# A four-layer graph network on one core: own rows gathered inside layer 2's tile loop, and the check of the softmax's bound moved ahead of the last tile's closing

## The chip, the core and the metric

The kernel runs on 1 core of one Trainium2 chip. A core has four engines that compute, TensorE (PE in the profile, with PEld for its weight loads), VectorE (DVE), ScalarE (ACT) and GpSimd (POOL), and SyncE (SP), which here only starts transfers. Each engine works through its own list of instructions in order; semaphores hold an instruction until what it needs is there. The metric is the device time of one execution in microseconds (us), and a kernel's time is the median over its runs. Beside the timed runs there is one execution under the profiler; all durations and starts below come from that one, and starts count from the beginning of its span.

## The reference

3125 nodes with 128 features, 100000 edges sorted by their destination. Four layers, each `x = layernorm(x + layer(x))`. The change lies in the third of them, which the kernel calls layer 2, an attention over each node's incoming edges with 4 heads of 32 features:

```python
Q = (x @ Wq).reshape(n, H, HD); K = (x @ Wk).reshape(n, H, HD); V = (x @ Wv).reshape(n, H, HD)
attn = jnp.sum(Q[dst] * K[src], axis=-1) * SCALE + edge_attr @ We
attn = jnp.where(attn >= 0, attn, 0.2 * attn)
attn_exp = jnp.exp(attn - jnp.max(attn))
attn_sum = jax.ops.segment_sum(attn_exp, dst, num_segments=n)
attn_norm = attn_exp / jnp.maximum(attn_sum[dst], 1e-12)
agg = jax.ops.segment_sum(V[src] * attn_norm[:, :, None], dst, num_segments=n)
agg = agg.reshape(n, H * HD) @ Wo + bo
return relu(jnp.concatenate([x, agg], axis=1) @ Wm + bm)
```

Two things in it matter here. The exponential is taken against one maximum over all edges and heads, and the sum has a floor of 1e-12. The layer behind it, layer 3, is again an attention over the edges, in which each edge uses a key that depends on its type (8 types) and on its source node.

## The kernel before

**Tiles.** The nodes are ordered by their number of incoming edges and cut into 25 tiles (`NT`) of 128, one node per partition. Tile t holds `CAP[t]` edge slots per node, from 57 for tile 0, then 42, 40, 39 down to 21 for the last: 821 slots in all (`NS`). The slots are worked on in chunks of 8 (`W`), and several chunks make a segment with one softmax update (`segments`); tile 0 has two segments. Edges beyond a node's slots would be handled by an overflow loop (`behind`, L641 to L667), a loop with a trip count that is read at run time (L647). With this data it makes no trip. Its head (L648) is a barrier of all engines, at which outstanding transfers are waited for as well.

**Tables.** The layer before leaves two tables in DRAM: `xq_tab`, for each node its own features and its query (256 floats), and `kv_tab`, key and value (256 floats). `pay_sb` holds for every slot the source node, the edge's type and its three attributes; it is loaded at L1124 in one transfer of 2463 KB on SP's queue. `xqb` keeps own features (`xb`) and queries (`qb`) of all 25 tiles in SBUF; layer 3 uses both halves as layer 2 has rewritten them.

**Gathers.** Every gather is an indirect DMA issued by POOL (helper `gather`, L90): one instruction fetches 128 rows, one per partition, from a table by a column of indices. Scatters (`scatter`, L93, through `put`, L736) go the same way.

**Layer 2, in the order of the source** (L1118 to L1277):

- `accb`, the accumulator of all tiles, is cleared (L1134), and the 25 gathers of own rows into `xqb` follow (L1135 to L1136).
- The overflow loop (`behind(wp, behind2)`), and behind it the loads of the weights.
- For each tile: `query` (L706) copies the tile's queries into PSUM. For each chunk `rows2` issues 8 gathers into `kv`, which has 8 buffers, multiplies keys by queries on DVE (`qk`, L1143) and sums over the features (L1144). `biased` (L1147 to L1155) adds the edges' bias, `softmax` (L670 to L687) updates a running maximum `m` and sum `l` of each node and head, `faded` (L691) rescales the accumulator, and `weigh` (L693 to L701) multiplies the values by the weights (`msg`, L696), sums over the slots (`u`, L700) and adds to the accumulator (L701).
- `closing(t, rl)` (L1186 to L1204): accumulator over sum (`an`), transposed on PE (L711), times `wo` (`o_ps`, L1194), own features transposed (L711), both times `wm` (`h_ps`, L1199 and L1200), `y` (L1202, L1203) and the layernorm (L717 to L729), which writes the new features into `xb`.
- `table3(t)` (L1206 to L1224): queries, keys and values of layer 3, and for each of the 8 edge types the transformed key (`e_ps`, L1221; `rows`, L1222); one scatter of 128 rows of 8 KB into `ktv_tab` ends it (L1224, by L93).
- After all tiles the check. The kernel normalizes by a maximum per node and head instead of the one over everything, so the floor of 1e-12 might apply in the reference where it doesn't here. The check takes the maximum of `m` over everything (`mx_all`, transposed on PE at L1252, `top`, L1254), scales the sums to it (`f`, L1256 and L1257; L1260), counts the sums that lie under the floor (`few`, L1262 to L1266, by a matmul over the partitions) and reads the count into a register of every engine (L1268, L1269). If it is above 0 (L1270), all tiles are closed again. With this data it is 0.

Layer 3 (from L1279) has the same shape: memsets, an overflow loop with its barrier, then gathers from `ktv_tab` and a loop over the tiles.

**What sets the order.** The source gives the data flow, and tile pools give the buffers (two of each name unless `bufs` says otherwise; in PSUM one). A scheduler places each engine's instructions; their order on an engine is then fixed and need not be that of the source.

Of the kernel before, what the change touches and what calls it, by code (L numbers as in the profile page):

```python
# [18 lines left out]
P = 128  # L19
N = 3125  # L20
NT = 25
# [38 lines left out]
def segments(t):  # L60

    cs = chunks(t)
    n = -(-len(cs) // 5)
    runs = [cs[i * len(cs) // n:(i + 1) * len(cs) // n] for i in range(n)]
    return [(run[0][0], sum(run[-1]), run) for run in runs]
# [10 lines left out]
def tile_gnn(ctx, tc, a, out):  # L76
    nc = tc.nc
    V, A, G, T = nc.vector, nc.scalar, nc.gpsimd, nc.tensor
# [10 lines left out]
    def gather(dst, table, idx, **kw):  # L89
        return G.indirect_dma_start(out=dst, out_offset=None, in_=table, in_offset=indirect(idx), **kw)  # L90
# [10 lines left out]
    ident = const.tile([P, P], F32, name="ident")  # L101
# [5 lines left out]
    ones = const.tile([P, P], F32, name="ones")  # L107
# [355 lines left out]
    od = Order("d", order_d)  # L463
# [21 lines left out]
    with tc.tile_pool(name="srcp", bufs=1) as sp, tc.tile_pool(name="srcq", bufs=2, space=PSUM) as ps:  # L485
# [8 lines left out]
        for t in range(NT):  # L494
# [245 lines left out]
    xq_tab = dram.tile([NP, 2 * D], F32, name="xq_tab")  # L740
# [7 lines left out]
    with tc.tile_pool(name="l0", bufs=2) as wp, tc.tile_pool(name="l0s", bufs=1) as sp, \  # L748
# [243 lines left out]
    with ExitStack() as ctx1, tc.tile_pool(name="l1", bufs=2) as wp, tc.tile_pool(name="l1s", bufs=1) as sp:  # L992
# [71 lines left out]
        ps1 = ctx1.enter_context(tc.tile_pool(name="l1p", bufs=1, space=PSUM))  # L1064
# [53 lines left out]
    H2 = 4  # L1118
    big = ctx.enter_context(tc.tile_pool(name="big", bufs=1))
    xqb = big.tile([P, NT, 2 * D], F32, name="xqb")  # L1120
# [4 lines left out]
    with tc.tile_pool(name="l2", bufs=2) as wp, tc.tile_pool(name="l2s", bufs=1) as sp, \  # L1125
# [6 lines left out]
        l = sp.tile([P, NT, H2], F32, name="l")  # L1132
        V.memset(l, 0.0)
        V.memset(accb, 0.0)  # L1134
        for t in range(NT):  # L1135
            gather(xqb[:, t, :], xq_tab, od.ids(t))  # L1136

        def rows2(qp, pl, n, lg):
            kv = wp.tile([P, W, 2 * D], F32, name="kv", bufs=8)
            for s in range(n):  # L1140
                gather(kv[:, s, :], kv_tab, pl[:, s, 0:1])
            qk = wp.tile([P, W, D], F32, name="qk")
            V.tensor_mul(qk[:, :n], kv[:, :n, :D], qp.unsqueeze(1).to_broadcast([P, n, D]))  # L1143
            V.tensor_reduce(lg, qk[:, :n].rearrange("p s (h d) -> p s h d", h=H2), AX.X, OP.add)  # L1144
            return kv
# [10 lines left out]

        def behind2(t, pl, mk, rl):
            lg = wp.tile([P, max(CAP), H2], F32, name="lg")
            kv = rows2(query(ps1, qb[:, t, :]), pl, W, lg[:, :W])
            biased(pl, W, lg[:, :W], mk)  # L1160
            ex = ps1.tile([P, max(CAP), H2], F32, name="ex")
            corr = softmax(wp, lg[:, :W], W, H2, m[:, t, :], l[:, t, :], ex[:, :W])
            faded(accb[:, t, :], corr, H2)
            weigh(wp, accb[:, t, :], kv[:, :, D:], ex[:, :W], W, H2)
# [21 lines left out]
        def closing(t, scale):  # L1186

            an = wp.tile([P, D], F32, name="an")
            V.tensor_tensor(an.rearrange("p (h d) -> p h d", h=H2),
                            accb[:, t, :].rearrange("p (h d) -> p h d", h=H2),  # L1190
                            scale.unsqueeze(2).to_broadcast([P, H2, D // H2]), op=OP.mult)
            aT = transposed(wp, ps1, an, "aT")
            o_ps = ps1.tile([P, P], F32, name="o_ps", tag="dense")
            T.matmul(o_ps, wo, aT, start=True, stop=True)  # L1194
            oT = wp.tile([P, P], F32, name="oT")
            A.activation(oT, o_ps, AF.Identity, bias=bo)
            xT = transposed(wp, ps1, xb[:, t, :], "xT")
            h_ps = ps1.tile([P, D], F32, name="h_ps", tag="dense")
            T.matmul(h_ps, xT, wm[:, 0, :], start=True, stop=False)  # L1199
            T.matmul(h_ps, oT, wm[:, 1, :], start=False, stop=True)  # L1200
            y = wp.tile([P, D], F32, name="y")
            V.tensor_add(y, h_ps, bm)  # L1202
            V.scalar_tensor_tensor(y, y, 0.0, xb[:, t, :], op0=OP.max, op1=OP.add)  # L1203
            layernorm(wp, xb[:, t, :], y, t)  # L1204

        def table3(t):  # L1206
# [16 lines left out]
            A.activation(rows[:, :, D:], qkv[:, 2 * D:].unsqueeze(1).to_broadcast([P, NET, D]), AF.Copy)  # L1223
            put(ktv_tab, od, t, rows.rearrange("p e f -> p (e f)"))  # L1224

        for t in range(NT):
            qp = query(ps1, qb[:, t, :])
            for s0, s1, run in segments(t):
                lg = wp.tile([P, max(CAP), H2], F32, name="lg")
                parts = []  # L1230
                for c0, w in run:
                    o = OFF[t] + c0
                    parts.append(rows2(qp, pay_sb[:, o:o + w], w, lg[:, c0 - s0:c0 - s0 + w]))
                n, o = s1 - s0, OFF[t] + s0
                biased(pay_sb[:, o:o + n], n, lg[:, :n], mask[:, o:o + n])
                ex = ps1.tile([P, max(CAP), H2], F32, name="ex")
                corr = softmax(wp, lg[:, :n], n, H2, m[:, t, :], l[:, t, :], ex[:, :n])
                faded(accb[:, t, :], corr, H2)
                for (c0, w), kv in zip(run, parts):
                    weigh(wp, accb[:, t, :], kv[:, :w, D:], ex[:, c0 - s0:c0 - s0 + w], w, H2)  # L1240

            rl = wp.tile([P, H2], F32, name="rl")
            V.tensor_scalar(rl, l[:, t, :], 1e-12, None, op0=OP.max)
            V.reciprocal(rl, rl)
            closing(t, rl)
            table3(t)


        mx = sp.tile([P, 1], F32, name="mx_all")
        V.tensor_reduce(mx, m, AX.XY, OP.max)  # L1250
        mt = ps1.tile([P, P], F32, name="tp")
        T.transpose(mt, mx.to_broadcast([P, P]), ident)  # L1252
        top = sp.tile([P, 1], F32, name="top")
        V.tensor_reduce(top, mt, AX.X, OP.max)  # L1254
        f = sp.tile([P, NT, H2], F32, name="f")
        V.tensor_scalar(f, m, top, None, op0=OP.subtract)  # L1256
        A.activation(f, f, AF.Exp)  # L1257
        has2 = sp.tile([P, NT, H2], F32, name="has2")
        V.tensor_scalar(has2, l, 0.0, None, op0=OP.is_gt)
        V.tensor_mul(l, l, f)  # L1260
        few = sp.tile([P, NT, H2], F32, name="few")
        V.scalar_tensor_tensor(few, l, 1e-12, has2, op0=OP.is_lt, op1=OP.mult)  # L1262
        few1 = sp.tile([P, 1], F32, name="few1")
        V.tensor_reduce(few1, few, AX.XY, OP.add)
        few_ps = ps1.tile([1, 1], F32, name="few_ps", tag="tp")
        T.matmul(few_ps, few1, ones[:, :1], start=True, stop=True)  # L1266
        fewi = sp.tile([1, 1], I32, name="fewi")
        V.tensor_copy(fewi, few_ps)  # L1268
        again = nc.values_load(fewi, min_val=0, max_val=NP * H2)  # L1269
        with tc.If(again > 0):  # L1270
            V.tensor_scalar(l, l, 1e-12, None, op0=OP.max)
# [78 lines left out]
```

## Time and profile before

| | |
|---|---|
| time, median of 3 runs | 5862.23 us |
| the runs | 5864.28, 5854.55, 5862.23 us |
| the profiled execution | 5814.11 us |
| its span | 5812.4 us |
| mean clock granted to TensorE | 0.588 of full speed |
| PE / PEld busy | 2236.2 us (38%) / 1363.8 us (23%) |
| ACT busy | 934.1 us (16%) |
| gathers of own rows in layer 2 | 25, from 3223.3 to 3253.4 us, 943 to 989 ns each |
| edge gathers of layer 2 | 821, from 3262.7 to 4503.6 us, median 947 ns |
| layer 3's edge gathers begin | 4592.45 us |

The page of a profile begins with the busy time of each engine. A chain of waits follows back from the last instruction: at each step to what released it, or to the instruction before it on its engine; "issue" in it is time in which an engine waited for nothing that the profile shows. Groups of instructions are given by line, engine, operation and tile, as `out<-in`; behind the bar stands the time that the engine was idle before them and what ended most of it. In a timeline each instruction has its start, its duration, engine, line and operation; the brackets hold the idle time of its engine just before and the releaser. The duration of an indirect DMA on POOL is that of making its descriptors; the data land later. The profiled execution is 48 us shorter than the median of the timed runs, so a difference of a few microseconds is read within one trace, not between a trace and a time.

### The profile page before, as it was taken

To read this page: it belongs to the slowest core of one execution; us is meant where nothing else is said; L and a number is where in the kernel's file an instruction comes from. 1 tells how busy PE (TensorE), PEld (TensorE's weight loads), DVE (VectorE), ACT (ScalarE), POOL (GpSimd) and SP (SyncE) were. 2 spreads that over 40 slices of the span, in tenths; PEclk is the share of its full clock that TensorE was granted. 3 is DMA by queue.
4 is the path that set the end of the run, shared out by engine and by line. 5 is a ranking of instruction groups with operands and counts; after the bars stand their busy time and mean duration, and the time that the engine had idled before them with its cause. 6 is when DMAs were issued, how large, how long until landed. Compare 5 with 4: busy or idle time off the path is not lost. (4 is left out here: it accounts for less than half of the span.)

```text
span 5812.4 us, 36204 instructions
## 1 busy us (share of the span) xinstructions
PE 2236.2 (38%) x10027; PEld 1363.8 (23%) x10027; DVE 3104.1 (53%) x6976; ACT 934.1 (16%) x2437; POOL 3074.3 (53%) x3136
## 2 busy tenths in 40 slices
PE   7165545555556556576658112222233200000000
PEld 5143333333334334344433001111111100000000
DVE  8354555554455446565652346565656455545555
ACT  1031222221222222222211001111111100000000
POOL 0555545545453544444640566566656366666664
PEclk9565556555665666566569555555555555555555
DMA  2423322322222222222335333333333233333332
GB/s 80 120 75 85 88 75 76 86 74 80 74 81 70 80 76 79 82 76 79 102 92 196 106 95 107 99 110 114 104 100 107 72 96 92 90 93 93 94 89 66
DMA packets 220239, 530.60 MB, mean 91 GB/s; under 512 B 65690, under 2 KB 112461, under 8 KB 215386
## 3 DMA queue, kind: packets, MB, share of 16 engines
q0 software_dynamic: 147968, 437.97, 26.6%
q1 hardware_dynamic: 72024, 89.90, 4.7%
q8 instruction: 87, 1.43, 0.1%
q14 instruction: 160, 1.30, 0.1%
HBM read 457.09 MB, written 70.63 MB: 91 GB/s over the span
## 5 line engine op out<-in xcount | busy, mean ns | idle before, releaser
L90 POOL DMA_INDIRECT hs<-h_tab,srcx x821 | 880.0, 1072 | 602.1 <-issue 448.7
L90 POOL DMA_INDIRECT kv<-kv_tab,pay_sb x821 | 782.1, 953 | 421.7 <-issue 239.5
L90 POOL DMA_INDIRECT kv<-ktv_tab,pay_sb x821 | 778.8, 949 | 332.3 <-issue 258.1
L90 POOL DMA_INDIRECT zs<-z_tab,rel x445 | 466.8, 1049 | 695.4 <-DVE az L810 303.3
L628 PE MATMUL c_ps<-c_ohs,c_ohd 128*128 128x128 bf16 x1300 | 334.3, 410 | 299.1 <-issue 110.3
L700 DVE TENSOR_REDUCE u<-msg 128x128 f32<-128x1024 f32 (+4 forms) x228 | 384.2, 1685 | 114.3 <-remote 69.6
L838 PE MATMUL zps<-oh,zq 128*128 128x512 bf16 x752 | 339.7, 516 | 88.3 <-DVE oh L834 80.1
L790 PE MATMUL lg<-yw,low 128*128 128x8 f32 x1642 | 306.4, 316 | 125.8 <-ACT low L788 81.6
L790 PEld LDWEIGHTS lg<-yw,low 128*128 128x128 f32 x1642 | 305.2, 276 | 162.8 <-ACT low L788 104.0
L628 PEld LDWEIGHTS <-c_ohd 128*128 128x128 bf16 x1300 | 187.2, 147 | 431.7 <-issue 256.2
L1295 DVE TENSOR_TENSOR qk<-kv,qp 128x1024 f32<-128x1024 f32 (+4 forms) x114 | 126.4, 1109 | 289.1 <-DMA kv<-ktv_tab,pay_sb 242.8
L623 DVE TENSOR_TENSOR c_ohs<-c_ends,c_up 128x1024 bf16<-128x1024 bf16 (+4 forms) x193 | 118.9, 616 | 248.0 <-remote 111.8
L696 DVE TENSOR_TENSOR msg<-kv,ex 128x1024 f32<-128x1024 f32 (+4 forms) x228 | 249.1, 1104 | 0.0
L604 ACT ACTIVATE c_oha<-c_oha,srclo 128x50 bf16<-128x50 bf16 (+2 forms) x821 | 201.5, 327 | 258.8 <-DVE c_oha L600 189.5
L850 DVE TENSOR_TENSOR hs<-hs,t_ps 128x408 f32<-128x408 f32 x141 | 74.5, 528 | 300.2 <-remote 193.0
L787 DVE TENSOR_TENSOR low<-pre,h1T 128x512 f32<-128x512 f32 (+1 forms) x215 | 141.3, 660 | 166.9 <-PE pre L843 76.1
L630 ACT ACTIVATE c_sb<-c_ps 128x512 bf16<-128x512 f32 (+1 forms) x175 | 96.5, 552 | 802.2 <-remote 363.0
L1143 DVE TENSOR_TENSOR qk<-kv,qp 128x1024 f32<-128x1024 f32 (+4 forms) x114 | 126.1, 1107 | 181.6 <-DMA kv<-kv_tab,pay_sb 173.1
L849 PE MATMUL t_ps<-zw,zT 128*128 128x136 f32 x752 | 153.7, 338 | 151.1 <-issue 105.1
L711 PE MATMUL tp<-ident,xk 128*128 128x128 f32 x100 | 42.3, 423 | 426.7 <-DVE xk L1211 88.6
L711 PE MATMUL tp<-ident,an 128*128 128x128 f32 x25 | 11.5, 461 | 434.5 <-DVE msg L696 174.3
L788 ACT ACTIVATE low<-low 128x512 f32<-128x512 f32 (+1 forms) x215 | 128.9, 606 | 274.7 <-DVE low L787 246.1
(394 smaller groups left out, 5252.7 us busy)
## 6 DMA issues: line engine op xcount, KB each, us to landing
c_tab<-c_sb SPq DMA_DIRECT2D x25, 768.0 KB
cs<-c_tab SPq DMA_DIRECT2D x6, 3200.0 KB
hs<-h_tab,srcx POOLq DMA_INDIRECT x821
kv<-kv_tab,pay_sb POOLq DMA_INDIRECT x821
kv<-ktv_tab,pay_sb POOLq DMA_INDIRECT x821
rb<-rel_tab SPq DMA_DIRECT2D x47, 256.0 KB
zs<-z_tab,rel POOLq DMA_INDIRECT x445
h_tab<-h SPq DMA_DIRECT2D x25, 132.0 KB
```

The lines of the kernel that those rows point to most:

```text
L90: return G.indirect_dma_start(out=dst, out_offset=None, in_=table, in_offset=indirect(idx), **kw)
L604: A.activation(oha[:, s, 0, :], oha[:, s, 1, :], AF.Copy, scale=srclo[:, o:o + 1])
L628: T.matmul(cps[:, j * P:(j + 1) * P], ohd[:, :, nb * j + i], ohs[:, :, nb * j + i], start=(i == 0), stop=(i == nb - 1))
L696: V.tensor_tensor(msg[:, :n, :].rearrange("p s (h d) -> p s h d", h=heads), val.rearrange("p s (h d) -> p s h d", h=heads), ex.unsqueeze(3 ...
L700: V.tensor_reduce(u, msg[:, :n, :].rearrange("p s d -> p d s"), AX.X, OP.add)
L787: V.tensor_add(low[:, :k], pre[:, :k], h1T.unsqueeze(1).to_broadcast([P, k, P]))
L788: A.activation(low[:, :k], low[:, :k], AF.Relu)
L790: T.matmul(lg_ps[:, s, :], low[:, s, :], yw8, start=True, stop=True)
L838: T.matmul(z, w, oh[:, i], start=(whole and i == 0), stop=(whole and i == NK - 1))
L849: T.matmul(t_ps[:, s, :], zT[:, (s0 + s) * P:(s0 + s + 1) * P], zw[:, D:], start=True, stop=True)
L1143: V.tensor_mul(qk[:, :n], kv[:, :n, :D], qp.unsqueeze(1).to_broadcast([P, n, D]))
L1295: V.tensor_mul(qk[:, :n], kv[:, :n, :D], qp.unsqueeze(1).to_broadcast([P, n, D]))
```

## The change

The 25 gathers of own rows leave the place in front of the overflow loop. In the tile loop the rows of tile 0 are gathered ahead of the loop, and those of tile t + 1 behind the query of tile t; the body of the overflow loop, which makes no trip here, gets its own gather. The check becomes a function and is called in the last tile's turn, behind its sums and in front of its `closing`; its operations are the same.

```diff
         V.memset(accb, 0.0)
-        for t in range(NT):
-            gather(xqb[:, t, :], xq_tab, od.ids(t))
-
...
         def behind2(t, pl, mk, rl):
             lg = wp.tile([P, max(CAP), H2], F32, name="lg")
+            gather(xqb[:, t, :], xq_tab, od.ids(t))
             kv = rows2(query(ps1, qb[:, t, :]), pl, W, lg[:, :W])
...
+        def check():
+
+            mx = sp.tile([P, 1], F32, name="mx_all")
+            V.tensor_reduce(mx, m, AX.XY, OP.max)
+            mt = ps1.tile([P, P], F32, name="tp")
+            T.transpose(mt, mx.to_broadcast([P, P]), ident)
...
+            T.matmul(few_ps, few1, ones[:, :1], start=True, stop=True)
+            fewi = sp.tile([1, 1], I32, name="fewi")
+            V.tensor_copy(fewi, few_ps)
+            return f, fewi
+
+        gather(xqb[:, 0, :], xq_tab, od.ids(0))
         for t in range(NT):
             qp = query(ps1, qb[:, t, :])
+            if t + 1 < NT:
+                gather(xqb[:, t + 1, :], xq_tab, od.ids(t + 1))
             for s0, s1, run in segments(t):
...
             V.reciprocal(rl, rl)
+            if t == NT - 1:
+                f, fewi = check()
             closing(t, rl)
             table3(t)
 
-
-        mx = sp.tile([P, 1], F32, name="mx_all")
-        V.tensor_reduce(mx, m, AX.XY, OP.max)
...
-        fewi = sp.tile([1, 1], I32, name="fewi")
-        V.tensor_copy(fewi, few_ps)
         again = nc.values_load(fewi, min_val=0, max_val=NP * H2)
```

More of the change, by code (lines that the diff above doesn't have):

```diff
@@ L1224, in table3 @@
             put(ktv_tab, od, t, rows.rearrange("p e f -> p (e f)"))
+        def check():
[3 more added lines that the diff above has]
+            T.transpose(mt, mx.to_broadcast([P, P]), ident)
+            top = sp.tile([P, 1], F32, name="top")
+            V.tensor_reduce(top, mt, AX.X, OP.max)
+            f = sp.tile([P, NT, H2], F32, name="f")
+            V.tensor_scalar(f, m, top, None, op0=OP.subtract)
+            A.activation(f, f, AF.Exp)
+            has2 = sp.tile([P, NT, H2], F32, name="has2")
+            V.tensor_scalar(has2, l, 0.0, None, op0=OP.is_gt)
+            V.tensor_mul(l, l, f)
+            few = sp.tile([P, NT, H2], F32, name="few")
+            V.scalar_tensor_tensor(few, l, 1e-12, has2, op0=OP.is_lt, op1=OP.mult)
+            few1 = sp.tile([P, 1], F32, name="few1")
+            V.tensor_reduce(few1, few, AX.XY, OP.add)
+            few_ps = ps1.tile([1, 1], F32, name="few_ps", tag="tp")
+            T.matmul(few_ps, few1, ones[:, :1], start=True, stop=True)
[3 more added lines that the diff above has]
+        gather(xqb[:, 0, :], xq_tab, od.ids(0))
         for t in range(NT):
             qp = query(ps1, qb[:, t, :])
+            if t + 1 < NT:
+                gather(xqb[:, t + 1, :], xq_tab, od.ids(t + 1))
             for s0, s1, run in segments(t):
@@ L1244, in tile_gnn @@
             V.reciprocal(rl, rl)
+            if t == NT - 1:
+                f, fewi = check()
             closing(t, rl)
             table3(t)
-        mx = sp.tile([P, 1], F32, name="mx_all")
-        V.tensor_reduce(mx, m, AX.XY, OP.max)
[L1251 to L1266, printed above, removed]
-        fewi = sp.tile([1, 1], I32, name="fewi")
-        V.tensor_copy(fewi, few_ps)
         again = nc.values_load(fewi, min_val=0, max_val=NP * H2)
```

## The prediction

> **What bounds the kernel now.** I read the page's head first, then the timeline of the start of layer 2, the wait of its barrier, and the timelines of the places that the diff touches. All times are us from the start of the span.
>
> ```profile
> span 5812.4 us, 36204 instructions
> ...
> PE 2236.2 (38%) x10027; PEld 1363.8 (23%) x10027; DVE 3104.1 (53%) x6976; ACT 934.1 (16%) x2437; POOL 3074.3 (53%) x3136
> ...
> POOL 12%; DVE 12%; issue 12%; another core or an unknown queue 5%; PE 2%; DMA 1%; ACT 1%; DVEq 0%; POOLq 0%; ACTq 0%
> ...
> L90 POOL DMA_INDIRECT kv<-kv_tab,pay_sb x821 | 782.1, 953 | 421.7 <-issue 239.5
> ```
>
> No engine is full: POOL, which issues every gather, and DVE have 53% each, and the chain that ended last goes back and forth between them. A layer-2 gather costs POOL 0.953 us and 0.3 us up to the next one (239.5 us over 786), 1.25 us in all. The change touches the start of layer 2 and its last tile, so I look there.
>
> The timeline of layer 2's start (start, duration, engine, line, what; in brackets the idle time before it and its releaser):
>
> ```profile
> 3222.52 0.32 SPq L1124 DMA_DIRECT2D pay_sb<-pay_tab  x1
> 3223.15 2.73 DVE L1134 MEMSET accb<- 128x3200 f32 x1 [3.16 <-DMA kv_tab<-kv]
> 3223.33 0.99 POOL L90 DMA_INDIRECT xqb<-xq_tab,node_d  x1 [174.73 <-issue]
> 3224.63 0.97 POOL L90 DMA_INDIRECT xqb<-xq_tab,node_d  x1 [0.30 <-issue]
> ...
> 3253.44 0.96 POOL L90 DMA_INDIRECT xqb<-xq_tab,node_d  x1 [0.30 <-issue]
> ...
> 3259.56 0.94 DVE L1149 TENSOR_TENSOR eb<-pay_sb,we 128x384 f32<-128x384 f32 x2 [33.56 <-issue]
> ...
> 3262.68 0.94 POOL L90 DMA_INDIRECT kv<-kv_tab,pay_sb  x1 [8.28 <-DVE eb L1149]
> ```
>
> The 25 gathers of own rows run from 3223.33, one per 1.25 us, to 3254.4. DVE has been idle for 33.6 us when it goes on at 3259.56, and the first edge gather starts at 3262.68. What held them is the barrier at the head of the overflow loop (L648), in the view of waits; and the stretches beside it show when the big load of `pay_sb` has drained (length, then busy us and counts of PE, PEld, DVE, ACT and POOL, PE's clock, the DMA share, GB/s):
>
> ```profile
> SPq L648 <- DMA xqb<-xq_tab,node_d: 35.1, 1, 35.1
> ```
> ```profile
> 3230.00:3232.00 2.00, 0.00 (x0) 0.00 (x0) 0.00 (x0) 0.00 (x0) 1.55 (x2) 0.50 0.87 328
> ...
> 3240.00:3256.00 16.00, 0.00 (x0) 0.00 (x0) 0.00 (x0) 0.00 (x0) 11.04 (x12) 0.50 0.36 107
> ```
>
> SP's queue waits 35.1 us for the landing of own rows. `pay_sb` (2463 KB, issued at 3222.52) holds the DMA engines at 0.87 until about 3232, after which they fall to the 0.36 that own rows alone make: it has landed by about 3232.
>
> **Part 1, own rows.** The order of instructions says more than the source. The scheduler does not place one gather per tile: behind the barrier POOL now issues 12 gathers of own rows, 57 edge gathers, 1 of own rows, 32 edge gathers, 12 of own rows, 50 edge gathers, then tile 0's scatter (L93). Before, the scatter followed 139 edge gathers. Everything behind that scatter keeps its order on POOL, and DVE, ACT, PE and SP keep theirs in the whole loop but for the last tile. The number of gathers that run is the same.
>
> Removed: the barrier's wait for own rows. What is late next is `pay_sb`, which POOL needs for its indices: 3232, plus what POOL takes to its first DMA. The bounds are 0.3 us, its usual step, and the 3.1 us by which it left the barrier later than DVE (3262.68 − 3259.56); I take 0.9, nearer the first, because the exit can be done while the load still runs. First own-row gather at 3232.9 (3232.3 to 3235.1). Twelve at 1.25 make 15.0: the first edge gather starts at 3247.9 instead of 3262.68, **14.8 us earlier** (12.6 to 15.4). If the barrier holds for `pay_sb` as well, add the 6.5 us that lie between about 3256.2 (own rows landed: 3253.44 plus some 2.7) and 3262.68: 3238.5, so 9.2 earlier; that is the lower bound.
>
> Added in the stream: one gather behind the 57th, 1.25 us, on the path, since tile 0's products wait for data (see the line at 3365.78 below, 7.39 us of waiting): left **13.5 us**. Twelve more behind the 89th, 15.0 us on POOL: edge gather 90 and later come 1.5 us later than before, and POOL reaches the scatter at 3438.3 instead of 3436.8. This I cost at nothing, and its cover is this:
>
> ```profile
> 3365.78 1.22 DVE L1143 TENSOR_TENSOR qk<-kv,qp 128x1024 f32<-128x1024 f32 x1 [7.39 <-DMA kv<-kv_tab,pay_sb]
> ...
> 3380.64 0.32 DVE L674 TENSOR_REDUCE mx<-lg 128x4 f32<-128x96 f32 x1 [1.11 <-DVE accb L701]
> ...
> 3383.44 0.16 DVE L676 TENSOR_TENSOR mn<-m,mx 128x4 f32<-128x4 f32 x1 [1.11 <-DVE u L700]
> ...
> 3455.58 0.99 POOL L93 DMA_INDIRECT ktv_tab<-rows,node_d  x1 [19.12 <-issue]
> 3459.96 0.96 POOL L90 DMA_INDIRECT kv<-kv_tab,pay_sb  x1 [3.39 <-DVE msg L696]
> ```
>
> 3365.78 is the last product that waits for data. The products behind it start long after their last gather: the 97th is issued at 3262.68 + 96 × 1.25 = 3382.7, its product starts at 3419.6; the 115th at 3405.2, its product at 3442.6. With some 2.7 for landing, DVE 13.5 earlier and the data 1.5 later, 19 of these 37 us are left. And POOL sat idle 19.1 us before the scatter, which waits for tile 0's rows: of these 1.5 + 13.5 go, 4 stay. So the scatter goes at 3442 instead of 3455.6, and from there the old order runs 13.5 us early. Without this cover, part 1 is worth −13.5 + 15 = +1.5.
>
> Against such a move speaks the Trainium skill, page "SBUF — State Buffer", section "SBUF: two separate sides": while DVE runs an operation in a two-port mode, GpSimd can't write the descriptors of its DMAs; a transfer of 620 ns alone took 3100 ns beside a DVE copy. By that rule each of the 13 gathers that now stand among DVE's work would cost up to 2.5 us more, an estimate of 32 us. The rows do not show it for the issue: own-row gathers with DVE idle took 943 to 989 ns, edge gathers beside DVE's work 947 in the median.
>
> **Part 2, the check.** The six operations of the check move from behind the last tile's closing to between tile 23's rows (L1222) and tile 24's `y` (L1202); on PE its two matmuls now stand ahead of the transpose of `an`.
>
> ```profile
> 4559.67 0.27 PE L711 MATMUL tp<-ident,an 128*128 128x128 f32 x1
> 4559.87 0.69 DVE L1222 TENSOR_TENSOR rows<-e_ps,mu 128x512 f32<-128x512 f32 x1 [0.79 <-PE e_ps L1221]
> ...
> 4577.09 0.28 DVE L1254 TENSOR_REDUCE top<-tp 128x1 f32<-128x128 f32 x1
> ...
> 4578.93 0.19 PE L1266 MATMUL few_ps<-ones,few 128*1 128x1 f32 x2 [2.38 <-DVE few L1264]
> ...
> 4592.45 0.99 POOL L90 DMA_INDIRECT kv<-ktv_tab,pay_sb  x1 [13.57 <-issue]
> ```
>
> Removed at the end: nothing that counted. The check ended at 4579.3, while POOL went on to layer 3 only after tile 24's scatter, issued at 4577.92, had landed (about 4583). That landing is the cover on the old side; I book 0, at most 0.3 of gain. Added: PE waits in order for `few`, so the transpose of `an` at 4559.67 comes after it. `top` can start when DVE is through with the rows, 4560.5; from `top` to the matmul of `few` took 4578.93 − 4577.09 = 1.84, that matmul 0.19: `an` at 4562.6, **2.9 us later**, with `o_ps`, `y`, the layernorm, table and scatter of tile 24 behind it and layer 3 behind them. Bounds: 2.0 (if DVE's part goes ahead of the last rows, 0.7 saved, and 0.2 at each end) and 4.5 (if the table load for the exponential, 1.28 as L706's at 3259, falls into the chain). Nothing hides it: POOL's last edge gather starts at 4503.6.
>
> **Sum.** −13.5 + 2.9 = −10.6 (at best −15.4 + 1.25 + 2.0 − 0.3 = −12.4; at worst −9.2 + 1.25 + 4.5 = −3.5). The profiled execution took 5814.1 with 1.7 outside its span; it would take 5803.5. It is 48.1 us shorter than the median, 5862.23, of three runs that lie 10 us apart; I take the difference to the median: 5851.6, so **5852**, and 5846 to 5859 for this case alone.
>
> **Rivals.** From 3379 to 3456 DVE is slow for a reason that no wait shows: instructions that need each other follow after 1.1 us (the two lines above with 1.11), elsewhere after a few hundredths. The stretches come back about every two tiles and end when POOL comes out of a pause. My case takes them to move along with DVE.
>
> B, the gain is eaten before the scatter: if the slow stretch ends by POOL's own work (164 gathers before the scatter now end 1.5 us later), DVE's lead is lost. For it: the stretch lasted until POOL's next DMA. Against it: POOL had nothing to do for 19 us and DVE was still slow, so it was POOL that waited. Price +1.5 + 2.9 = +4.4: 5867.
>
> C, the slower side: the stretch begins by a count of POOL's unbroken run. It ran 3262.68 to 3379 without a pause before the stretch, 116 us. Now the run begins with own rows at 3232.9, and 116 us later is 3349, before the 22 instructions that DVE ran from 3366.9 to 3378.7 at full pace, then at about 3353 to 3365. Slowed by 1.11 each they cost 24.4: −13.5 + 24.4 + 2.9 = +13.8, 5876. It decides as soon as all 22 are slowed; half of them leave +1.6. For it: the stretch falls into POOL's longest run. Against: own rows ran without a pause before as well, and nothing of DVE's stood beside them.
>
> D, the change does not do what it says: own rows are not spread one per tile, 24 of 25 still go in two lumps ahead of tile 0's scatter. That is in the sum already; if the barrier found the first ones outstanding all the same, part 1 would be 0 and the time +2.9: 5865, counted with B.
>
> **How the numbers follow.** My case 0.55, B with D 0.18, C 0.27. A measurement of this kernel can tell about 0.2% (11.7 us) from no change: 5850.5 is the bound below, 5874 above. My case stands at its lower bound; with three runs 10 us apart I give it 0.30 for faster and 0.25 for the same. B gives 0.17 to the same and 0.01 to slower, C all to slower: 0.30, 0.42, 0.28. The range goes from 5841 (my case's best, −12.4, less half of the runs' 10 us and a little for a shorter slow stretch) to 5880 (C and 4 for the runs), leaving some 2 in 10 outside, most of it above.
>
> **What would show it.** Right: the barrier's wait for own rows is gone; the first edge gather starts near 3248; tile 0's scatter near 3442 with some 4 us of idle before it; the transpose of `an` of tile 24 waits about 3 us for `few`; layer 3's first gather near 4582. Wrong: a first gather after 3255 (the barrier waits for `pay_sb`); the rows at 1.1 us beginning before 3360 (C); the scatter at 3455 or later (B). The most that I rest on is that slow stretches move with DVE and do not change in length or number over the 24 tiles that follow; one more or one less would outweigh everything in the sum.

## The result, and the profile after

The changed kernel takes 5855.7 us in the median (12 runs, 5837.45 to 5871.62), the kernel before beside it 5855.6 (12 runs, 5844.36 to 5864.28): ratio 1.0004, 95% interval 0.9991 to 1.0018. So nothing moved by as much as 0.2%. The two profiled executions, 5814.1 before and 5852.6 after, differ by 38 us, but 25.3 of these lie ahead of layer 2, in code that both share. What the change did must be read inside the layer, and I count from one instruction that both have at the same place, the load of `pay_sb` (3222.52 before, 3247.84 after).

The head of the page after: span, busy time, chain, and the group of the edge gathers.

```profile
span 5850.6 us, 36140 instructions
...
PE 2197.8 (38%) x9956; PEld 1350.6 (23%) x10027; DVE 3108.0 (53%) x6976; ACT 935.5 (16%) x2438; POOL 3073.3 (53%) x3136
...
DVE 13%; POOL 12%; issue 11%; another core or an unknown queue 5%; PE 1%; DMA 1%; ACT 0%; DVEq 0%; POOLq 0%; ACTq 0%; SPq 0%
...
L90 POOL DMA_INDIRECT kv<-kv_tab,pay_sb x821 | 779.8, 950 | 430.6 <-issue 240.9
```

Nothing in it tells the kernels apart. The timeline of the layer's start does (start, duration, engine, line, what; in brackets the idle time before it), with the barrier's wait from the view of waits:

```profile
3247.84 0.32 SPq L1124 DMA_DIRECT2D pay_sb<-pay_tab  x1
...
3258.13 0.99 POOL L90 DMA_INDIRECT xqb<-xq_tab,node_d  x1 [184.36 <-issue]
...
3272.12 0.95 POOL L90 DMA_INDIRECT xqb<-xq_tab,node_d  x1 [0.30 <-issue]
3273.37 0.95 POOL L90 DMA_INDIRECT kv<-kv_tab,pay_sb  x1 [0.30 <-issue]
```
```profile
SPq L648 <- DMA pay_sb<-pay_tab: 7.8, 1, 7.8
```

The 35.1 us of waiting for own rows are gone; SP waits 7.8 for the load instead. The first edge gather starts 25.5 us after the load was issued, before 40.2: 14.6 earlier. Then POOL's timeline around tile 0's scatter (L93) and its pauses, the time in brackets:

```profile
3462.32 0.95 POOL L90 DMA_INDIRECT kv<-kv_tab,pay_sb  x1 [0.30 <-issue]
3467.66 0.99 POOL L93 DMA_INDIRECT ktv_tab<-rows,node_d  x1 [4.39 <-issue]
3480.46 0.96 POOL L90 DMA_INDIRECT kv<-kv_tab,pay_sb  x1 [11.80 <-remote]
...
3524.03 0.95 POOL L90 DMA_INDIRECT kv<-kv_tab,pay_sb  x1 [13.78 <-DVE msg L696]
...
3592.91 1.00 POOL L93 DMA_INDIRECT ktv_tab<-rows,node_d  x1 [0.30 <-issue]
```

The scatter comes 219.8 after the load, before 233.1: the lead is 13.2. But POOL now pauses 11.8 us behind it and 13.8 us once more at the 164th edge gather. By tile 2's scatter, the last line, the lead is gone (345.1 against 344.3), and tiles 6 to 13 come within 0.2 us of before. POOL's pauses from its first edge gather to the 203rd, by its timeline: 19.1 + 3.4 + 13.8 = 36.3 before, 4.4 + 11.8 + 13.8 + 6.2 = 36.2 after. They have moved; they have not become less.

DVE's slow stretch, in which instructions that need each other follow 1.1 us apart, starts at the same instructions in both traces: 156.7 us after the load before, 142.8 after, 13.9 earlier. It does not end at the same place. These rows of DVE's timelines show the end of it before, and its first long idle time and its end after:

```profile
3455.54 0.24 DVE L680 COPY m<-mn 128x4 f32<-128x4 f32 x1 [3.89 <-remote]
3455.69 1.21 DVE L1144 TENSOR_REDUCE lg<-qk 128x32 f32<-128x1024 f32 x1
```
```profile
3392.72 0.28 DVE L700 TENSOR_REDUCE u<-msg 128x128 f32<-128x128 f32 x1 [1.07 <-DVE mx L674]
...
3522.25 0.15 DVE L722 TENSOR_SCALAR bn_sd<-bn_mv 128x1 f32<-128x1 f32 x1 [1.07 <-DVE accb L691]
3522.32 0.32 DVE L684 TENSOR_REDUCE sm<-ex 128x4 f32<-128x160 f32 x1
```

Before, it ends 233 us after the load, beside the scatter of tile 0; after, it runs on to 274. It has grown from some 77 us to some 132.

At the layer's end, the timeline of the last tile:

```profile
4588.81 0.69 DVE L1220 TENSOR_TENSOR rows<-e_ps,mu 128x512 f32<-128x512 f32 x1 [0.94 <-PE e_ps L1219]
...
4591.27 0.19 PE L1243 MATMUL few_ps<-ones,few 128*1 128x1 f32 x2 [2.38 <-DVE few L1241]
...
4591.70 0.33 PE L711 MATMUL tp<-ident,an 128*128 128x128 f32 x1 [0.24 <-DVE fewi L1245]
...
4595.08 0.29 DVE L1200 TENSOR_TENSOR y<-h_ps,bm 128x128 f32<-128x128 f32 x1 [3.44 <-PE h_ps L1198]
```

The transpose of `an` follows 2.9 us behind tile 23's last rows instead of 0.2 ahead of them, because PE waits for `few` first: 3.1 later. `y` follows 6.3 behind them instead of 2.3, 4.0 later. Layer 3's first edge gather comes 1379.1 us after the load, before 1369.9: 9.2 later, of which more below.

### The profile page after: what moved, and what is told of

It reads as the page before. It is cut to its first block, busy times and chain, and to the rows that moved or that the text cites. A ratio compares the mean times of both kernels' runs of the same rounds, so it can differ in the third digit from the quotient of the medians.

```text
span 5850.6 us, 36140 instructions
## 1 busy us (share of the span) xinstructions
PE 2197.8 (38%) x9956; PEld 1350.6 (23%) x10027; DVE 3108.0 (53%) x6976; ACT 935.5 (16%) x2438; POOL 3073.3 (53%) x3136
## 5 line engine op out<-in xcount | busy, mean ns | idle before, releaser
L790 PE MATMUL lg<-yw,low 128*128 128x8 f32 x1642 | 298.4, 311 | 125.0 <-ACT low L788 88.3
L838 PE MATMUL zps<-oh,zq 128*128 128x512 bf16 (+1 forms) x693 | 308.9, 510 | 86.6 <-DVE oh L834 70.4
L628 PEld LDWEIGHTS <-c_ohd 128*128 128x128 bf16 x1300 | 186.8, 147 | 474.7 <-issue 282.0
L1211 PE MATMUL p_ps<-wqkv,xkT 128*128 128x384 f32 x200 | 156.4, 883 | 45.5 <-ACT xkT L713 27.9
```

The lines of the kernel that those rows point to most:

```text
L628: T.matmul(cps[:, j * P:(j + 1) * P], ohd[:, :, nb * j + i], ohs[:, :, nb * j + i], start=(i == 0), stop=(i == nb - 1))
L790: T.matmul(lg_ps[:, s, :], low[:, s, :], yw8, start=True, stop=True)
L838: T.matmul(z, w, oh[:, i], start=(whole and i == 0), stop=(whole and i == NK - 1))
L1211: T.matmul(p_ps, xkT, wqkv[:, k, :], start=(k == 0), stop=(k == NTY - 1))
```

## The experiments

Four theories were named as they came up. COVER is the prediction's own: own-row gathers beside DVE's slow stretch are free. PAUSE: DVE's slow stretch lasts until POOL makes a long pause, and the earlier start took that pause away. FIXED: the layer's pace doesn't depend on its start. LATE DATA, later sharpened to STREAM: POOL's stream of DMAs sets the layer. The first four runs shared a chip on which the kernel before takes 5854 us; the others ran on three more chips, and on all of these it takes 5148 to 5149. So each ratio is taken beside runs of the kernel before on the same chip, and traces are compared on the same level.

**e1, the gathers alone.** The changed kernel with the check back at the end:

```diff
-            if t == NT - 1:
-                f, fewi = check()
             closing(t, rl)
             table3(t)
+        f, fewi = check()
```

> The own-row gathers moved as in the changed kernel, the check left at the end. I read the layer's length in the profile, from the issue of the load of pay_sb to layer 3's first edge gather: 1369.9 us before, 1379.1 changed. In the changed trace the first edge gather came 14.6 us earlier against the load of pay_sb and tile 0's scatter 13.2 earlier, but tile 1's scatter 8.4 later and tile 2's 0.8 later: the gain is gone within two tiles. Three theories. PAUSE: DVE's slow stretch lasts as long as POOL issues without a long pause; the earlier start shortened POOL's pause at tile 0's scatter, so the stretch ran on through tile 1. LATE DATA: the 25 own-row gathers ahead of the scatter make POOL late for tile 3's data. FIXED: the layer's pace is set by something that does not move with its start, and any earlier start is given back. All three expect the changed kernel's pattern here (first edge gather at 25.5 after the load, tile 2's scatter within 2 us of 344.3) and a layer shorter than the changed one by the price of the check, 2.9 by my sum: 1376, and a time within 0.2% of before.

Measured: first edge gather at 25.5, tile 2's scatter at 345.8, layer 1380.4, ratio 0.9997 (0.9986 to 1.0008). The pattern is that of the changed kernel, so it belongs to the gathers. The layer did not get shorter: from one execution to the next the last ten tiles differ by up to 9 us with the same order (tile 23's scatter at 1338.8 in before and at 1348.2 in e2, and the two kernels differ only behind it), so what the check costs is read from tile 23 on. Of the 9.2 us by which the changed kernel's layer was longer in its trace, 3.6 are there by tile 23's scatter, and the rest comes behind it.

**e2, the check alone.** The kernel before, with `check()` called ahead of the last `closing`.

> The check moved ahead of the last tile's closing, the own-row gathers left in front of the barrier. All theories: nothing changes up to tile 23's scatter (1338.8 after the load of pay_sb); the transpose of tile 24's an waits for the check's count. By my sum tile 24's scatter comes 2.9 us later (2.0 to 4.5) against tile 23's, 19.5 instead of 16.6 us behind it; the changed trace has 20.4. Layer 1370 + 3 to 5, time +3 to +5 us, under 0.1%, not to be told from before by the times.

Measured: ratio 1.0012 (0.9997 to 1.0027). `an` is 2.9 behind tile 23's last rows and `y` 6.4, as in the changed kernel; from those rows to layer 3's first edge gather it takes 39.9. Two expected numbers were missed: tile 24's scatter came 24.1 behind tile 23's and not 19.5 (without the check ahead this distance lies between 16.6 and 20.4 in the traces), and the layer took 1386.7 and not 1373 to 1375. In the three traces with the check ahead the stretch from tile 23's last rows to layer 3's first edge gather takes 38.1, 39.9 and 37.7, mean 38.6; in the ten others up to e8 32.6 to 37.9, mean 35.0. The means differ by 3.6 us, and that is the price taken here for the check ahead; the two groups touch, so a single trace can't give it.

**e3, own rows one per tile.** As e1, with POOL's order held by edges that only order, and no wait:

```diff
-            if t + 1 < NT:
-                gather(xqb[:, t + 1, :], xq_tab, od.ids(t + 1))
...
                     parts.append(rows2(qp, pay_sb[:, o:o + w], w, lg[:, c0 - s0:c0 - s0 + w]))
+                    if c0 == 0 and t + 1 < NT:
+                        behind_of(gather(xqb[:, t + 1, :], xq_tab, od.ids(t + 1)), order[-1])
```

> As e1, but POOL's order is held so that the own rows of tile t+1 are really gathered behind the first chunk of tile t: 4 of them stand ahead of tile 0's scatter instead of 25, and the order of all other instructions is that of e1. First edge gather at about 11.6 us after the load of pay_sb (28.5 earlier than before), POOL through its 143 gathers at about 190. PAUSE: tile 0's scatter at about 206, so POOL pauses 16 us or more as before, the slow stretch ends there and the lead stays: layer 1343 to 1350, time 20 to 27 us shorter than before (0.35 to 0.45%). LATE DATA: the same, 25 us shorter. FIXED: the layer stays at 1370 to 1376 and the time within 3 us of before.

Measured: first edge gather 11.5 after the load, 28.7 earlier than before; tile 0's scatter at 206.5 as expected, tile 2's at 323.6, 20.7 earlier. So FIXED falls: a lead can live. But then it melts tile by tile (tile 8: 15.1, tile 12: 8.4, tile 16: 1.4, tile 20: −3.4), and the time is that of before (0.9992, 0.9979 to 1.0005). From tile 2 to tile 16 the loop holds 15 more own-row gathers, and 19.3 us are lost, 1.3 for each. That is the step of POOL from one gather to the next, 1.25, and little else. The layer took 1378.4, where PAUSE and LATE DATA had expected some 25 less than before.

**e4, a pause.** As e1, with 80 memsets of 128x96 on POOL behind tile 0's scatter and all other orders held (those lines are left out):

```diff
+                for i in range(80):
+                    held.append(G.memset(scr, 0.0))
+                    behind_of(held[-1], (held[-2:-1] or [p])[0])
```

> As e1, but POOL does 80 small memsets of 96 columns (some 15 to 19 us, no DMA) between tile 0's scatter and its next edge gather; the order of everything else on all engines is held as in e1. PAUSE: the added dead time ends DVE's slow stretch at about 240 us after the load instead of 275; tile 1's scatter comes at 290 to 297 instead of 311.6, and the layer is 10 to 14 us shorter than e1's although POOL does more. LATE DATA: the pause makes tile 3's data still later: tile 1's scatter at 311 or later, the layer longer by up to 17. FIXED: tile 2's scatter stays within 2 us of 344.3 and the layer as in e1.

Measured: ratio 1.0037 (1.002 to 1.0053); tile 1's scatter at 322.5, tile 2's at 364.7, 18.9 later than e1's, and it stays so to tile 16 (18.3). The memsets took 36 us, not 15 to 19, so the price that PAUSE put on this run is not tested fairly. Its timelines of POOL and DVE still tell something (the second of POOL's rows holds 64 memsets in a run):

```profile
3463.71 0.19 POOL L1337 MEMSET scr<- 128x96 f32 x1
...
3484.40 15.04 POOL L1337 MEMSET scr<- 128x96 f32 x64 [0.52 <-POOL scr L1337]
3499.99 0.97 POOL L190 DMA_INDIRECT kv<-kv_tab,pay_sb  x1 [0.54 <-issue]
```
```profile
3511.75 1.22 DVE L1249 TENSOR_TENSOR qk<-kv,qp 128x1024 f32<-128x1024 f32 x1 [23.31 <-DMA kv<-kv_tab,pay_sb]
3512.89 0.32 DVE L1261 TENSOR_TENSOR lg<-lg,mask 128x160 f32<-128x160 f32 x1
```

The first 16 memsets have 0.5 to 2.3 us of idle time between them, mostly 1.2; from 3484 on, 241 us after the load, 64 follow one another, and from about there DVE runs at full pace too. So the slow stretch is not DVE's alone, and it did end in the pause, as PAUSE expected (about 240, in e1 275). But the layer got longer, for DVE then stood 23.3 us for data. The 36.3 us of memsets stand where e1 has pauses of 11.8 us behind the scatter and, at the 164th gather, of 14.5, which are gone here; the pause at the 203rd gather is 8.6 longer. The next edge gather came 24.6 later than in e1, and 18.9 of them stayed. So a block on POOL is not free, and it is not paid in full.

**e5, a plain load.** From here on STREAM stood: the layer's length is POOL's start, plus 1.25 us for each of its DMAs wherever it stands, plus pauses of a constant sum (for DMAs that are moved; in e4, where POOL itself was held, the pauses shrank). Then it helps to take DMAs out of POOL's stream. `place_d` keeps each node's rank, which the sort has computed anyway. Against the kernel before, with the lines for `place_d` and the overflow loop left out:

```diff
-                nc.sync.dma_start(xq_tab[j * P:(j + 1) * P], xq)
+                unordered("xq", scatter(xq_tab, place_d[:, j:j + 1], xq), "nodes differ")
...
-        for t in range(NT):
-            gather(xqb[:, t, :], xq_tab, od.ids(t))
...
+        nc.sync.dma_start(xqb[:, 0, :], xq_tab[:P])
+        nc.sync.dma_start(xqb[:, 1:, :], xq_tab[P:].rearrange("(t p) f -> p t f", p=P))
```

> A version meant to be faster: layer 1 writes xq_tab by 25 scatters of POOL, which idles there, each node at its place in the sorted order; layer 2 then fetches own rows with two plain loads on SP's queue behind the barrier, and POOL's 25 own-row gathers are gone from layer 2. The check stays at the end. The runs so far: one per tile started the edge gathers 28.7 us earlier, had 21.3 left at tile 1's scatter and 20.7 at tile 2's, and lost 1.2 us per tile after that, as many as its own-row gathers cost POOL. STREAM (the theory that I now hold): the layer's length is POOL's start, plus 1.25 us for each of its DMAs wherever they stand, plus pauses that come back with the same size; so here the first edge gather at about 10.5 us after the load of pay_sb instead of 40.2, nothing given back later, tile 2's scatter at 314 to 318 instead of 344, tile 20's 27 to 30 earlier than before's 1244.5, the time 25 to 30 us (0.4 to 0.5%) shorter, less what the scatters cost at the end of layer 1, 0 to 3. COVER (my prediction's own reading, in which DMAs beside DVE's slow stretch are free): 28 earlier as well. FIXED, which e3 speaks against: no change.

Measured: ratio 0.9985 (0.9976 to 0.9993), 7 us. The first edge gather comes 10.5 after the load, tile 2's scatter at 285.8 (on this level of chip 315.2 before, see below). But the tail of layer 1, from its first write of `xq_tab` to the load of `pay_sb`, takes 146 us, in e7 beside it 124: the tile `xq` has two buffers, and DVE waits until a scatter has landed (20.6 us in 12 waits).

**e6 and e7, fewer own rows, and all of them in front.** As e1, with the first 13 own-row gathers (e6) or all 25 (e7) in one run ahead of the first edge gather. For e7:

```diff
-        gather(xqb[:, 0, :], xq_tab, od.ids(0))
+        for t in range(25):
+            gather(xqb[:, t, :], xq_tab, od.ids(t))
         for t in range(NT):
             qp = query(ps1, qb[:, t, :])
-            if t + 1 < NT:
-                gather(xqb[:, t + 1, :], xq_tab, od.ids(t + 1))
```

In e6 it is `range(12)`, with the gather of tile 12's rows behind tile 0's query, and `V.memset(xqb[:, 13:, :], 0.0)` follows the clearing of `accb`; in the trace the 13 gathers stand in one run. e6 leaves out the own rows of twelve tiles, so it doesn't compute the layer: it only shows what twelve gathers cost.

> As e1, with the own rows of tiles 0 to 12 in one run of 13 gathers ahead of the first edge gather and those of tiles 13 to 24 left out (zeros from one memset of DVE stand in their place); POOL's order is else that of e1. Against e1 the first edge gather comes 1.25 later, and the 12 gathers behind the 89th are gone. STREAM: tile 2's scatter at 345.8 + 1.25 - 1.25 - 15 = about 331, tiles 3 to 13 the same 15 us earlier, the time 12 to 15 us shorter than e1's. COVER: those 12 cost nothing in e1, so tile 0's scatter comes at about the same time and tile 2's within 2 us of 346. PAUSE: POOL is through 15 us earlier, so its pause at tile 0's scatter is 19 us again, the slow stretch ends there and the lead of 13 us stays: tile 1's scatter at about 291, tile 2's at 331; it agrees with STREAM here and not in e7.

> As e1, with all 25 own-row gathers in one run behind the barrier and ahead of the first edge gather; all other orders are those of e1. First edge gather at 10.3 + 25 x 1.25 = 41.5 us after the load of pay_sb, 16 later than e1 and 1.4 later than before. STREAM: where the 25 stand does not matter, tile 2's scatter within 2 us of e1's 345.8, the time that of e1 within 3 us. COVER: DVE starts 16 us later than in e1, so everything comes 13 to 16 later than in e1 if e1 had a real lead; since e1 lost its lead by tile 2, this reading has no number of its own there and would have tile 0's scatter at 234 to 236. PAUSE: POOL's pause at tile 0's scatter is 19 us as before, the slow stretch ends there, tile 1's scatter at about 305 as before and not at 312 as in e1.

Measured, on the same chip: e7 has its first edge gather at 41.8 and tile 2's scatter at 316.0, ratio 1.0002 (0.9991 to 1.0013). e6 has them at 26.2 and 299.7, tile 20's scatter 17.7 earlier than e7's, ratio 0.9973 (0.9962 to 0.9984). Twelve gathers fewer are 16 us less, or 1.3 each. By the times it is 15.3 us, where STREAM expected 12 to 15. The numbers that were expected for the scatters came from the first chip and do not apply to this one; the kernels before and after on this level follow.

**The kernels before and after once more, and e3.**

> The kernel before, for its profile beside the next runs. The last three runs were made on a chip on which it takes 5149 us instead of 5855, and their traces show no slow stretch of DVE. On such a chip STREAM expects the layer (from the load of pay_sb to layer 3's first edge gather) at about 1220 us, 1.4 less than with all own rows in front (1221.4), the first edge gather at 40.2 and tile 2's scatter at 314.6. On a chip like the first: 1370 to 1380, 40.2 and 344.3.

> The changed kernel. STREAM: first edge gather at 25.5 us after the load of pay_sb, 14.6 earlier than before, and all of it given back by POOL's 13 own-row gathers among tiles 0 to 2: tile 2's scatter 0.5 to 1.5 later than before's on either chip, tile 23's within 3, and 4 more for the check at the end; time +5 us, under 0.1%. COVER (my prediction): with no slow stretch the cover that I booked is gone as well, part 1 is worth +1.5 by its own words. PAUSE, in which the lead is lost only because a slow stretch runs on: on a chip without slow stretches the lead of 13 us stays.

> Own rows one per tile, as in e3. STREAM: first edge gather at 11.5, the lead of 28.7 given back by 1.25 us for each of the 24 own-row gathers in the loop: tile 2's scatter 25 earlier than before's, tile 12's about 12 earlier, tile 23's level with before's within 3; time within 3 us of before. PAUSE on a chip without slow stretches: the lead stays, 25 us.

Measured on one chip, e7 on another of the same level (us after the load of `pay_sb`):

| | first edge gather | scatter 0 | scatter 2 | scatter 8 | scatter 16 | scatter 20 | ratio to before, interval |
|---|---|---|---|---|---|---|---|
| before | 40.4 | 214.8 | 315.2 | 618.4 | 951.6 | 1102.6 | 1.0 (0.9991 to 1.001) |
| changed | 25.7 | 216.3 | 316.0 | 619.9 | 953.2 | 1103.7 | 1.001 (1.0001 to 1.0019) |
| e7, 25 in front | 41.8 | 216.3 | 316.0 | 620.1 | 953.6 | 1104.0 | 1.0002 (0.9991 to 1.0013) |
| e3, one per tile | 12.0 | 190.2 | 292.7 | 603.6 | 947.9 | 1103.7 | 1.0004 (0.9995 to 1.0013) |
| e8, plain load | 10.6 | 185.0 | 285.2 | 588.9 | 922.4 | 1072.7 | 0.994 (0.9926 to 0.9954) |

The three middle rows hold the same 25 gathers at three sets of places, and all end level, 1.1 to 1.4 us behind before. The lead of e3 shrinks from 28.4 at the first edge gather to 22.5 at scatter 2, behind 5 more own-row gathers, and to −1.1 at scatter 20, behind all 24: 1.2 for each. There is no slow stretch in these traces, so PAUSE, which needs one to lose the lead, falls as the reason of the loss on this level: the changed kernel loses it here as well, at the second lump of twelve and ahead of scatter 0. Three of STREAM's numbers were a little off: e3's lead at scatter 2 is 22.5 and not 25, at tile 12 8.6 and not 12, and the changed kernel reaches tile 23's scatter 4.0 us ahead of before, where at most 3 either way was expected.

POOL's pauses bear STREAM out on both levels. Counted as idle time beyond the usual 0.3 us, from the first edge gather to tile 20's scatter, they make 38.2 to 39.3 us in the traces of before, changed, e3, e5, e6, e7 and e8 on this level. On the first chip they make 182.5 to 186.8 in before, changed, e1, e2 and e3, and 35.0 to 37.0 of that lie ahead of tile 2's scatter. Why they come back with the same sum there, no run shows. For before on this level the rest of the 1062.2 us between the two is 812 steps of POOL at 1.26 us. That a start, steps and pauses add up is arithmetic; what the traces add is that the pauses keep their sum when gathers move. The page and the waits of DVE in layer 2 of the kernel before on this chip (us in total, times, longest), and its POOL at tile 0's scatter:

```profile
span 5143.4 us, 36133 instructions
...
L90 POOL DMA_INDIRECT kv<-kv_tab,pay_sb x821 | 783.3, 954 | 297.7 <-issue 238.0
```
```profile
DVE qk L1143 <- DMA kv<-kv_tab,pay_sb: 355.8, 60, 12.6
```
```profile
3010.91 0.95 POOL L90 DMA_INDIRECT kv<-kv_tab,pay_sb  x1 [0.30 <-issue]
3012.16 1.00 POOL L93 DMA_INDIRECT ktv_tab<-rows,node_d  x1 [0.30 <-issue]
```

DVE waits 355.8 us for gathered data, and of the 297.7 us that POOL is idle before edge gathers, 238.0 are its own 0.3 between two instructions. The 19.1 us of idle time before the scatter, on which the prediction put its twelve free gathers, are 0.30 here.

**e8, the plain load with 8 buffers.**

```diff
-                xq = wp.tile([P, 2 * D], F32, name="xq")
+                xq = wp.tile([P, 2 * D], F32, name="xq", bufs=8)
```

> As e5, with 8 buffers instead of 2 for the tile that layer 1's scatters read. In e5 layer 2 was some 27 us shorter than with the gathers, but the tail of layer 1 (from its first write of xq_tab to the load of pay_sb) took 146 us instead of 124, since a buffer came free only when its scatter had landed. With 8 buffers the tail should be 124 to 128 and the time 25 us shorter than before: ratio 0.994 to 0.997.

> The kernel of the run before once more, in case this call falls to a chip like the first. STREAM on a chip where the kernel before takes about 5855 us: the first edge gather at 10.5 us after the load of pay_sb, tile 2's scatter at 314 to 318 instead of 344.3, the time 25 to 32 us shorter than before (0.4 to 0.55%). On a chip where it takes about 5149: ratio 0.993 to 0.995 as in the run before.

Measured: 5117.5 us beside 5148.5, ratio 0.994 (0.9926 to 0.9954); once more, on another chip of that level, 5117.9 beside 5148.3, 0.9945 (0.9931 to 0.9958). On a chip like the first it was not run. Its timeline:

```profile
2800.19 0.32 SPq L1126 DMA_DIRECT2D pay_sb<-pay_tab  x1
...
2810.74 0.98 POOL L90 DMA_INDIRECT kv<-kv_tab,pay_sb  x1 [12.22 <-issue]
2810.76 0.32 SPq L1250 DMA_DIRECT2D xqb<-xq_tab  x1
2811.14 0.42 SPq L1251 DMA_DIRECT2D xqb<-xq_tab  x1
```

The tail of layer 1 takes 125.0 us, as expected. The edge gathers start 10.6 after the load, 29.8 earlier than before, and at scatter 20 29.9 are left. This is what the changed kernel was to have and could not: here the 25 gathers have left POOL's stream, there they have changed their places in it. On the same chip the changed kernel takes 5152.9 us, so it beats both, by 0.6 and 0.7%.

## Why the prediction was right, and where not

**Time and sign.** 5852 was forecast, −10.6 against 5862.2; the result is 5855.7, which is +0.1 against a base that came to 5855.6 with more runs. The time lies in the range and the forecast stood at the lower bound of "the same", but the sum's −10.6 is not what happened. The 6.6 us by which three runs overstated the base hid most of the difference. That the forecast time lies so close to the measured one is luck.

**The start.** First own-row gather 10.4 after the load by the sum, 10.3 measured; first edge gather 25.4, measured 25.5. The barrier did wait for `pay_sb`, but its exit was not paid behind it, as the sum chose; the sign that the prediction gave for such a wait, a first gather after 3255, did not come with it (the first edge gather is at 3248.0 in that count). One gather on the path: lead 13.5 at scatter 0, measured 13.2. POOL's idle time there: 4, measured 4.4. All of this held.

**The twelve gathers "cost at nothing".** This step failed. The cover was worked out correctly up to scatter 0 and assumed to hold from there on, "the old order runs 13.5 us early". It ran 13.2 early at scatter 0 and 0.8 late at scatter 2. POOL's idle time before the scatter was no spare time: POOL waits for buffers that DVE frees, DVE for rows that POOL fetches, and on the first chip the sum of POOL's pauses came back, 36.3 and 36.2 us, at other places. On the other chips that idle time isn't there at all. The sign named for the end of the layer failed too: layer 3's first gather was to come near 4582 and came, in the count of before, at 4601.6. The working even held the right price, "Without this cover, part 1 is worth −13.5 + 15 = +1.5": measured +0.8 at scatter 2, and 0.8 to 1.6 on the other chip. In POOL's stream it is the difference of two starts: before, the 25 gathers began 0.8 after the load and the barrier's exit cost 8.3, so the first edge gather came at 40.2; after, with all 25 counted, it would be 10.3 + 25 × 1.25 = 41.6, as in e7.

**The slow stretch.** The prediction said that it rests most on slow stretches that move with DVE and keep their length. This one moved, by 13.9 us, but it grew from some 77 to some 132 us. On the first chip the longer stretch and POOL's returning pauses come together, and no run there parts them. On the other chips there is no stretch and the lead is lost all the same, so the loss doesn't need it.

**The check.** 2.9 forecast with bounds 2.0 and 4.5: `an` 3.1 later, `y` 4.0, some 3.6 by layer 3's first gather. The mechanism was right. The term left out is PE's clock behind the wait: `y` is 0.9 later than `an` alone explains, and `o_ps` takes 0.80 us at a granted clock of 0.50 instead of 0.49 at 1.00.

**The rivals.** B had nearly the measured price, +4.4 against 0.8 + 3.6, by another way: on the first chip the lead was intact at the scatter and lost behind it; on the other chips it was lost ahead of it, with no slow stretch. C's slow stretch did not begin by a count of POOL's run: it began at the same instructions of DVE as before, 13.9 us earlier like them (142.8 us after the load instead of 156.7), and the 22 instructions ahead of it still ran at full pace. The lead at scatter 0 shows that nothing was lost up to there. D was right in the words: 24 of 25 own rows go in two lumps.

**The range of the case alone.** Its lower end, 5846, is 4 us below the best sum that is worked out, 5862.2 − 12.4 = 5849.8, and no reason is given.

**DMAs beside DVE's work.** Against the rule of the Trainium skill's page "SBUF — State Buffer" ("SBUF: two separate sides"), the prediction followed the rows. The 13 own-row gathers among DVE's work took 0.94 to 0.97 us in the trace after, those ahead of it 0.94 to 1.13: no sign of the rule's cost. Whether any operation of DVE beside them runs in the mode that the rule is about, no trace shows.

## What to carry to other kernels

Idle time of an engine that waits for another in a loop is not cover: before a moved instruction is booked at nothing, ask whether that engine's whole stream (start, count times step, pauses) gets shorter. In this kernel POOL only issues DMAs in the loop: moving one within its stream wins what the place allows once and pays its step again later; taking it out of the stream wins. And a lead should be followed for two or three rounds of the loop, not to its first scatter.

## What the runs showed of the hardware

The same kernel took 5854 us on the first chip and 5148 to 5149 on three others, 12% less, at nearly the same granted clock of TensorE (0.588 and 0.600 in the traces of before). On the first chip DVE has the slow stretches, in which instructions that need each other follow 1.1 us apart; on the second there are none. In e4, on the first chip, POOL's first memsets stand mostly 1.2 us apart as well, until the stretch ends. The traces differ in one more way: a landing shows as 16 steps of a semaphore, and of these steps the first chip's trace of before holds 15463 and the second's 53933. Counted in stretches of 10 us against the gathers issued, the second has 15.8 to 16.1 for each up to 210 us after the load; the first has 16 in the first stretch of edge gathers, three and fewer from 30 us behind it up to the pause at tile 0's scatter, and 12 just behind that pause. Whether the missing records and the slow stretches have one cause, and whether the chip, its host or the recording makes it, wasn't tried.

PE's small matmuls come in two lengths, with the clock that is granted to them: in the layer the pair of `o_ps` took 0.79 to 0.80 us at 0.50 in 23 of the 25 tiles of before, and 0.49 us at 1.00 in the other two. The last tile is one of these two, with PE busy for 3.6 of the 4 us ahead of it; with the check ahead, PE waits 2.4 us for `few`, and the pair runs at 0.50. It isn't the check alone that decides it: in e6, without it and with PE as busy ahead, the same pair took 0.78 us at 0.59.
